# A four-layer graph network on one core: the bias of the norms on POOL, the normalisations split up, one set of transposes moved

## The chip, the cores and the metric

The kernel runs on one core of a Trainium2 chip. A core has a matrix engine (PE, with its weight loads shown apart as PEld), a vector engine (DVE), an activation engine (ACT), a general engine (POOL), and SyncE (SP), which starts transfers. Each has a queue of its own and takes its instructions strictly in the order in which they stand there; engines wait for each other by semaphores. The metric is the device time of one launch in microseconds (us), of which the median of three is taken.

## The reference, cut to what matters

There are 16 batches of 1024 nodes with 128 features (`x`) and an adjacency matrix of 1024 x 1024 (`adj`, about 1.6% of it non-zero). Four graph layers follow each other. Each begins with a norm over the 128 features and a ReLU, and adds its result to `x`:

```python
def _layernorm(x, axis=-1, eps=1e-5):
    m = jnp.mean(x, axis=axis, keepdims=True)
    v = jnp.var(x, axis=axis, keepdims=True)
    return (x - m) / jnp.sqrt(v + eps)

# --- layer 0 (adj_preln) ---
h = jnp.maximum(_layernorm(x, axis=-1), 0.0)
x = x + _L0_gnn_ref(h, adj, adj, L0_gnn_W, L0_gnn_b)
# --- layer 1 (adj_preln) ---
h = jnp.maximum(_layernorm(x, axis=-1), 0.0)
x = x + _L1_gnn_ref(h, adj, L1_gnn_W, L1_gnn_b)
# --- layer 2 (adj_preln) ---
h = jnp.maximum(_layernorm(x, axis=-1), 0.0)
x = x + _L2_gnn_ref(h, adj, ...)
# --- layer 3 (adj_preln) ---
h = jnp.maximum(_layernorm(x, axis=-1), 0.0)
x = x + _L3_gnn_ref(h, adj, L3_gnn_W, L3_gnn_a)
```

Layers 0 and 1 multiply by the adjacency matrix and a weight. Layer 2 is the heavy one: two rounds, each of which scores every edge with a small network over both of its nodes, adds up weighted messages, updates the nodes and normalises them (with weights `gamma` and `beta`; this norm ends the update and is not one of the four above). Layer 3 is an attention over the neighbours.

## The kernel before, in words

**Three lanes at once.** While the edge rounds of batch b run (the main lane, `main`), the attention of batch b - 1 is worked off beside them (`last`) and layers 0 and 1 of batch b + 1 (`first`), together with what main will need for it. Each lane is a Python generator that emits instructions and then yields a number; `weave` always takes next the lane that stands furthest behind, measured as the sum of its yielded numbers over its budget (`MAIN_US` 184, `FIRST_US` 115, `LAST_US` 70). A yield thus costs nothing on the chip: it only says where another lane's instructions may come in between, and a larger number puts the rest of the lane later. `layer0_own` is driven by a loop in `first` that charges 1.3 for every piece, whatever the piece itself yields. The framework beneath also moves an instruction ahead of others on its engine where it sees room for it, so the built order is near the emitted one but not the same. Once built, each engine's order is fixed.

**Data.** A batch's features are a tile of 128 partitions x 8 blocks x 128: 8 blocks of 128 nodes each. The edges are sorted into 36 buckets (pairs of node blocks, 28 off the diagonal and 8 on it), in 9 groups of 4. `build` makes four 0-1 matrices of a bucket (on, onT, om, omT) by a chain through one PSUM bank: PE turns (`pn`), ACT copies (`onT`), PE ranks (`pq`), DVE compares (`omT`), PE turns (`pm`), ACT copies (`om`). In the rounds, PE gathers by them (`pre`), ACT applies the ReLU (`hid`, line 1024), DVE keeps the remainder (line 1025), PE takes the dot products (`sc`), ACT the tanh (`srow`), and then DVE makes products (`val`) that PE scatters (`p`) and sums up as messages (`msg`).

**The norm.** `spread` makes the statistics of 8 blocks: 8 bn_stats on DVE and five small operations, then on POOL the power -1/2 of the variance (`rstd`, line 242). It returns the standard deviation's inverse, the *sum* of the two half means and a free row. `normal` makes from it the bias, -0.5 x sum x rstd, on DVE (line 249), and then normalises block by block on ACT, 8 activations with `rstd` as scale and the bias added (line 251). `pre_ln` emits the whole of it as one piece, then `transposed`: 8 transposes on PE (line 259) in two halves, each copied to SBUF by ACT (line 260). `layer0_own`, `layer1` and `layer3` begin with `pre_ln`; layer 2's norm is called in `first`, and `build` comes behind it. `update` uses `spread` too, for 4 blocks, and applies the result on DVE (lines 363 and 365).

So a norm is a chain DVE, POOL, DVE, ACT, PE, ACT, and each of its links stands in a queue with other lanes' work behind it. There are 64 such norms (4 in each of 16 batches) and 64 of `update`'s.

Of the kernel before, what the change touches and what calls it, by code (L numbers as in the profile page):

```python
# [13 lines left out]
AF = mybir.ActivationFunctionType  # L14
OP = mybir.AluOpType
# [36 lines left out]
def tile_four_gnn_layers(  # L52
# [22 lines left out]
    nc = tc.nc  # L75
# [106 lines left out]
    def flat(t):  # L182
        return t.rearrange("p t d -> p (t d)")

    def over_t(v, n=T):
        return v[:, None, :].to_broadcast([P, n, D])

    class Layers:
# [37 lines left out]
        def spread(self, src, name):  # L226

            n = src.shape[1]
            bn = self.small([P, T, 6], "bn", f"bn_{name}")[:, :n]
            for t in range(n):  # L230
                nc.vector.bn_stats(bn[:, t], src[:, t])

            st = self.small([P, 4, T], "stat", f"st_{name}")[:, :, :n]
            nc.vector.tensor_sub(st[:, 1], bn[:, :, 1], bn[:, :, 4])
            nc.vector.scalar_tensor_tensor(
                st[:, 2], bn[:, :, 2], D * LN_EPS, bn[:, :, 5], op0=OP.add, op1=OP.add
            )
            nc.vector.scalar_tensor_tensor(st[:, 1], st[:, 1], 0.25, st[:, 1], op0=OP.mult, op1=OP.mult)
            nc.vector.scalar_tensor_tensor(
                st[:, 1], st[:, 2], 1.0 / D, st[:, 1], op0=OP.mult, op1=OP.add  # L240
            )
            nc.gpsimd.tensor_tensor(st[:, 2], st[:, 1], half_neg[:, :n], op=OP.pow)  # L242
            nc.vector.tensor_add(st[:, 0], bn[:, :, 1], bn[:, :, 4])
            return st[:, 2], st[:, 0], st[:, 3]

        def normal(self, src, dst, func, name):

            rstd, mean2, less = self.spread(src, name)
            nc.vector.scalar_tensor_tensor(less, mean2, -0.5, rstd, op0=OP.mult, op1=OP.mult)
            for t in range(T):  # L250
                nc.scalar.activation(
                    dst[:, t], src[:, t], func, scale=rstd[:, t : t + 1], bias=less[:, t : t + 1]
                )

        def transposed(self, src, name, dst=None):
            dst = self.scratch(f"hT_{name}") if dst is None else dst
            for ts, ps in self.halves(f"tp_{name}"):
                for i, t in enumerate(ts):
                    nc.tensor.transpose(ps[:, i], src[:, t], ident)
                nc.scalar.activation(dst[:, ts[0] : ts[-1] + 1], ps, AF.Copy)  # L260
            return dst

        def pre_ln(self, xt, name, dst=None):

            h = self.scratch(f"h_{name}") if dst is None else dst
            self.normal(xt, h, AF.Relu, name)
            yield 2
            self.hT = self.transposed(h, name)
            yield 2

# [66 lines left out]
        def update(self, l, xf, xfT, msgT, dst, name):  # L337

            h2 = flat(self.scratch(f"h2s_{name}")).rearrange("p (k n) -> p k n", k=KB)
            for kb in range(KB):  # L340
                ps = self.one(f"h2_{name}_{kb}")
                for i, src in enumerate((xfT, msgT)):
                    nc.tensor.matmul(  # L343
                        ps, wu1_sb[:, l, i, kb * P : (kb + 1) * P], src,
                        start=(i == 0), stop=(i == 1),
                    )
                nc.scalar.activation(h2[:, kb], ps, AF.Relu, bias=bu1_sb[:, l, kb : kb + 1])
                yield 2
            new = self.scratch(f"xn_{name}")[:, :Q]
            ps = self.one(f"xn_{name}")  # L350
            for kb in range(KB):
                nc.tensor.matmul(
                    ps, wu2_sb[:, l, kb], h2[:, kb], start=(kb == 0), stop=(kb == KB - 1)
                )
            nc.scalar.activation(flat(new), ps, AF.Identity, bias=bu2_sb[:, l : l + 1])
            yield 2
            ps = self.one(f"tx_{name}").rearrange("p (t d) -> p t d", d=P)
            for t in range(Q):
                nc.tensor.transpose(ps[:, t], new[:, t], ident)
            nc.vector.tensor_add(dst, ps, xf)  # L360
            yield 1
            rstd, mean, _ = self.spread(dst, f"y_{name}")
            nc.vector.tensor_scalar(mean, mean, 0.5, None, op0=OP.mult)
            for t in range(Q):
                nc.vector.tensor_scalar(
                    dst[:, t], dst[:, t], mean[:, t : t + 1], rstd[:, t : t + 1],
                    op0=OP.subtract, op1=OP.mult,
                )
            yield 2
            nc.vector.tensor_mul(dst, dst, over_t(rows["gamma"][:, l], Q))  # L370
            nc.vector.tensor_add(dst, dst, over_t(rows["beta"][:, l], Q))
            yield 1
# [157 lines left out]
    class Edges:  # L530
# [197 lines left out]
        def first(self, b):  # L728
            s = self.next = Batch()
            lane, name = self.a, f"{b}"  # L730
            xt = self.work.tile([P, T, D], F32, tag="x", name=f"x_{b}")
            nc.sync.dma_start(xt, x[b].rearrange("(t p) d -> p t d", p=P))
            for _ in lane.layer0_own(xt, name):
                if b:
                    yield 1.3
            z, own = lane.z, lane.o
            yield 0


            s.adjT = self.dram.tile([N, N], F32, tag="adjT", name=f"adjT_{b}", bufs=3)  # L740
            has = self.work.tile([P, len(BUCKETS), P], FP8, tag="has", name=f"has_{b}", bufs=1)
            deg = self.work.tile([P, 2, T], F32, tag="deg", name=f"deg_{b}")
            rdeg = deg[:, 1]
            for t in range(T):
                at = self.load(
                    "a", adj[b, t * P : (t + 1) * P, :].rearrange("p (k n) -> p k n", n=P),
                    f"at_{b}_{t}",
                )
                ct = self.load("a", self.columns(adj[b], t), f"ct_{b}_{t}")
                turned = lane.scratch(f"tn_{b}_{t}")  # L750
                nc.scalar.activation(turned, at, AF.Copy, accum_out=deg[:, 0, t : t + 1])
                for ks, ps in lane.halves(f"tn_{b}_{t}"):
                    for i, k in enumerate(ks):
                        nc.tensor.transpose(ps[:, i], at[:, k], ident)
                    nc.scalar.activation(turned[:, ks[0] : ks[-1] + 1], ps, AF.Copy)
                    yield 1
                nc.sync.dma_start(self.columns(s.adjT, t), turned)
                parts = [(INDEX[t, t], t, t + 1)]
                if t + 1 < T:
                    parts.append((INDEX[t, t + 1], t + 1, T))  # L760
                for i, lo, hi in parts:
                    nc.vector.tensor_tensor(
                        has[:, i : i + hi - lo], ct[:, lo:hi], turned[:, lo:hi],
                        op=OP.logical_or, saturate=False,
                    )
                nc.vector.reciprocal(rdeg[:, t : t + 1], deg[:, 0, t : t + 1])
                lane.layer0_tile(t, ct, z, own, rdeg, name)
                yield 2
            lane.layer0_end(xt, own)
            self.count(s, has, name)  # L770
            yield 2
            yield from lane.layer1(
                xt, lambda t: self.load("a", self.columns(s.adjT, t), f"l1_{b}_{t}"), rdeg, name
            )
            s.xf = self.work.tile([P, T, D], F32, tag="xf0", name=f"xf0_{b}", bufs=1)
            yield from lane.pre_ln(xt, f"2_{name}", dst=s.xf)
            s.xT = self.kept(lane.hT, "xT", f"xT0_{b}")
            s.x = self.kept(xt, "x", f"xk_{b}")
            yield from self.build(s, has, name)

        def count(self, s, has, name):

# [49 lines left out]
                )  # L832
            return ps

        def build(self, s, has, name):

# [2 lines left out]
            for g, grp in enumerate(GROUPS):  # L841
# [3 lines left out]
                for i, tu in enumerate(grp):  # L845
                    b = INDEX[tu]
# [5 lines left out]
                rank = self.work.tile([P, Q, P], F16, tag="rank", name=f"rank_{name}_{g}")  # L852
                nc.scalar.activation(rank, pr, AF.Copy)
                yield 0.5
                for i, (t, u) in enumerate(grp):
                    nm = f"{name}_{t}_{u}"
                    on = self.rows_hot(s, t, u, nm)
# [6 lines left out]
                    for k in range(ck):  # L864
# [7 lines left out]
                        op=OP.is_equal, saturate=False,  # L872
# [570 lines left out]
```

## Time and profile before

| | |
|---|---|
| Time, median of 3 | 5407.02 us (5398.09 to 5412.55) |
| Span of the profiled run | 5411.4 us |
| Instructions | 113484 |
| POOL's power on 128x8 (line 242) | 64, 1.635 us in the median |
| The same on 128x4, in `update` | 64, 1.006 us |
| The bias on DVE (line 249) | 64, 0.167 us |
| A normalisation on ACT (line 251) | 512, 0.48 us |
| A steady batch | 328 us |

How it is read: the page gives each engine's busy time as a share of the span. Matmuls are pipelined and their ends are modelled, so a PE that is busy isn't necessarily at its peak; but where PE is *idle* in a kernel that PE bounds, time is lost. A group's row gives the line, the engine, the operation with its output and inputs, how often it ran, its busy time and mean, and behind the bar the idle time just before these instructions with what ended it. The windows give the busy time of each engine in a stretch.

### The profile page before, as it was taken

What the parts mean: (1) busy time and instruction counts of PE and PEld (TensorE: products, weight loads), DVE (VectorE), ACT (ScalarE), POOL (GpSimd) and SP (SyncE); (2) the same over time, 40 slices, a digit from 0 to 9 for tenths busy, and PEclk for the clock granted to TensorE, in tenths of its full rate; (3) what the DMA queues carried; (4) which work ended last, traced back from release to release, by engine and by line L of the source; (5) the groups of instructions that cost most, each with busy time, mean ns of one, the idle gap of its engine ahead of it and who ended that gap; (6) DMA issues with size and microseconds to landing.
All of it is one profiled execution on the core that took longest, in us unless ns stands there. A gap on an engine that the chain in (4) does not pass through costs nothing.

```text
span 5411.4 us, 113484 instructions
## 1 busy us (share of the span) xinstructions
PE 5012.4 (93%) x45109; PEld 3743.8 (69%) x45109; DVE 4288.8 (79%) x10567; ACT 3055.3 (56%) x6790; POOL 176.5 (3%) x137
## 2 busy tenths in 40 slices
PE   5999999999999999999999999999999999999986
PEld 4666767767776767767777677677767677677664
DVE  4776787877879788797877878778797787978876
ACT  4556464655646556465565656556465564655533
POOL 0000000000000000000000000000000000000000
PEclk8999999999999999999999999999999999999998
DMA  6242425243252423424234242432424334243121
GB/s 182 66 138 87 120 60 150 79 128 103 76 149 64 136 92 99 133 67 124 92 112 121 61 142 87 122 106 76 147 67 137 91 96 136 67 128 92 53 62 47
DMA packets 740139, 554.56 MB, mean 102 GB/s; under 512 B 32272, under 2 KB 686352, under 8 KB 739600
## 3 DMA queue, kind: packets, MB, share of 16 engines
q1 hardware_dynamic: 734496, 545.58, 33.6%
q8 instruction: 356, 5.83, 0.5%
q10 hardware_dynamic: 5104, 1.65, 0.1%
q14 instruction: 183, 1.50, 0.1%
HBM read 446.44 MB, written 100.66 MB: 101 GB/s over the span
## 4 chain that ended last, share of the span: by engine, by line
PE 61%; DVE 20%; ACT 10%; DMA 4%; POOL 2%; issue 2%; SPq 0%; ACTq 0%; POOLq 0%; DVEq 0%
PE pre L1008 15%; PE p L1120 7%; DVE val L1098 6%; PE nb L289 6%; PE msg L1137 5%; PE h L343 4%; PE hp L507 3%; PE bb L297 3%; PE sc L1041 3%; DVE hid L1025 3%; DMA at<-in_adj_dram 3%; PE pq L865 2%; PE pn L829 2%; POOL st L242 2%; ACT hid L1024 2%
## 5 line engine op out<-in xcount | busy, mean ns | idle before, releaser
L1024 ACT ACTIVATE hid<-pre 128x320 f16<-128x320 f32 (+1 forms) x2048 | 922.2, 456 | 713.5 <-PE pre L1008 679.5
L1025 DVE SCALAR_TENSOR_TENSOR hid<-pre,hid 128x320 f16<-128x320 f32 (+1 forms) x2048 | 1010.0, 505 | 262.7 <-ACT hid L1024 245.8
L1008 PEld LDWEIGHTS <-part 128*128 128x128 f16 x8192 | 752.7, 99 | 429.3 <-issue 211.4
L1008 PE MATMUL pre<-on,part 128*128 128x320 fp8e4 (+1 forms) x4096 | 966.6, 311 | 42.5 <-DVE hid L1025 32.3
L1008 PE MATMUL pre<-om,part 128*128 128x320 fp8e4 (+1 forms) x4096 | 979.0, 312 | 0.0
L1098 DVE TENSOR_TENSOR val<-onT,u 128x384 f32<-128x384 fp8e4 (+1 forms) x1152 | 603.3, 580 | 3.6
L1137 PE MATMUL msg<-upd,xf 128*128 128x128 f32 (+3 forms) x3008 | 591.8, 320 | 0.0
L1120 PE MATMUL p<-val,omT 128*128 128x128 f16 x6528 | 532.7, 219 | 31.6 <-DVE val L1098 27.2
L1120 PEld LDWEIGHTS <-omT 128*128 128x128 fp8e4 x6528 | 433.4, 96 | 109.6 <-issue 37.1
L1098 DVE TENSOR_TENSOR val<-omT,u 128x384 f32<-128x384 fp8e4 x896 | 442.7, 549 | 0.0
L1137 PEld LDWEIGHTS msg<-upd,xf 128*128 128x128 f32 x3008 | 411.6, 191 | 17.6 <-DVE upd L1128 0.9
L877 ACT ACTIVATE om<-pm 128x320 fp8e4<-128x320 f32 (+1 forms) x576 | 268.6, 466 | 274.5 <-PE pm L829 270.1
L1128 DVE SCALAR_TENSOR_TENSOR upd<-p,adj 128x512 f32<-128x512 f32 x512 | 349.0, 682 | 80.7 <-PE p L1120 76.7
L1120 PE MATMUL p<-val,onT 128*128 128x128 f16 x4480 | 370.9, 220 | 1.4 <-DVE upd L1128 1.4
L861 ACT ACTIVATE onT<-pn 128x384 fp8e4<-128x384 f32 (+1 forms) x576 | 298.4, 518 | 106.4 <-PE pn L829 98.4
L1062 ACT ACTIVATE srow<-sc,be_s,down 128x128 f32<-128x128 f32 (+2 forms) x512 | 256.3, 540 | 163.3 <-PE sc L1041 162.3
L507 PE MATMUL hp<-wh,e 128*128 128x129 f32 x2048 | 331.1, 287 | 16.7 <-DVE e L503 16.7
L1120 PEld LDWEIGHTS <-onT 128*128 128x128 fp8e4 x4480 | 305.2, 97 | 49.5 <-issue 14.9
L507 PEld LDWEIGHTS hp<-wh,e 128*128 128x128 f32 x2048 | 279.9, 195 | 51.5 <-issue 24.0
L1041 PE MATMUL sc<-hid,slide 128*32 128x320 f16 (+1 forms) x4096 | 272.4, 320 | 29.9 <-DVE hid L1025 28.5
L820 DVE TENSOR_SCALAR on<-far,wid 128x384 fp8e4<-128x384 f16 (+1 forms) x576 | 238.6, 427 | 60.0 <-PE pre L1008 52.2
L816 ACT ACTIVATE far<-iota_off,mid 128x384 f16<-128x384 f16 x448 | 275.6, 629 | 11.8 <-DVE on L820 11.3
(217 smaller groups left out, 8122.0 us busy)
## 6 DMA issues: line engine op xcount, KB each, us to landing
at<-in_adj_dram SPq DMA_DIRECT2D x128, 512.0 KB, 4.1
ct<-in_adj_dram SPq DMA_DIRECT2D x128, 512.0 KB, 4.5
adjT<-tn SPq DMA_DIRECT2D x128, 512.0 KB, 5.3
l<-adjT SPq DMA_DIRECT2D x128, 512.0 KB, 4.3
adj<-adjT SPq DMA_DIRECT2D x256, 256.0 KB, 3.5
a<-adjT SPq DMA_DIRECT2D x128, 384.0 KB, 3.2
adj<-adjT SPq DMA_DIRECT2D x448, 64.0 KB, 2.2
adj<-adjT SPq DMA_DIRECT2D x192, 128.0 KB, 2.9
```

The costliest lines, as they stand in the source:

```text
L289: nc.tensor.matmul(ps, mat[:, k], z[:, k], start=(k == 0), stop=(k == T - 1))
L507: nc.tensor.matmul(sums[:, t], e[:, i, t * P : (t + 1) * P], wh[:, k + i, : D + 1], start=False, stop=True, skip_group_check=True,)
L816: nc.scalar.activation(far[:, : ck * P], self.iota[t == u][:, : ck * P], AF.Abs, bias=s.mid[:, i : i + 1])
L861: nc.scalar.activation(onT, pn[:, : ck * P], AF.Copy, saturate=False)
L1008: nc.tensor.matmul(pre[:, :c], path.parts[node // Q][:, k, node % Q, v], hot[:, :c], start=(hot is on and k == 0), stop=(hot is om and k = ...
L1024: nc.scalar.activation(hid[:, 0, :c], pre[:, :c], AF.Relu)
L1025: nc.vector.scalar_tensor_tensor(hid[:, 1, :c], pre[:, :c], 0.0, hid[:, 0, :c], op0=OP.max, op1=OP.subtract)
L1041: ins = nc.tensor.matmul(self.sc[g * G : (g + 1) * G, : self.c], self.path.slide[:, self.l, G - 1 - r : 2 * G - 1 - r], self.hid[self.done ...
L1098: nc.vector.tensor_tensor(pair[:, i % 2, :ck], right[:, :ck], v.to_broadcast([P, ck, P]), op=OP.mult)
L1120: nc.tensor.matmul(self.ps[d][:, i], left[:, k], halves[:, k, :, h], start=(k, h) == terms[0], stop=(k, h) == terms[-1],)
L1128: nc.vector.scalar_tensor_tensor(upd, self.ps[d], S_SCALE, self.adj[:, d * Q : (d + 1) * Q], op0=OP.add, op1=OP.mult,)
L1137: nc.tensor.matmul(self.msg[h][:, (lo - h * Q) * P : (hi - h * Q) * P], self.xf[mb // Q][:, mb % Q], up, start=False, stop=True, skip_grou ...
```

## The change

It has three parts.

1. **The bias moves to POOL.** `spread` scales the sum of the means by -0.5 on DVE, so that it returns minus the mean; `normal` multiplies it by `rstd` on POOL, which has just made `rstd`, rather than on DVE, which would have to wait for it. `update` no longer scales the mean itself and adds it instead of subtracting.
2. **The normalisations are emitted by twos.** `normal` becomes a generator: it yields once behind the bias and once behind every second activation, so that other lanes' work can come between them. `pre_ln` passes these yields on.
3. **Layer 2's transposes wait.** In `first`, layer 2's norm is called directly, and its transposes (with the store of their result to DRAM) are handed to `build`, which emits them behind the first group of buckets. Batch 0, where nothing runs beside `build`, keeps its order. The copy of `x` to DRAM is emitted ahead of this norm.

```diff
@@ spread, normal
             nc.vector.tensor_add(st[:, 0], bn[:, :, 1], bn[:, :, 4])
+            nc.vector.tensor_scalar(st[:, 0], st[:, 0], -0.5, None, op0=OP.mult)
             return st[:, 2], st[:, 0], st[:, 3]
 
-        def normal(self, src, dst, func, name):
-
-            rstd, mean2, less = self.spread(src, name)
-            nc.vector.scalar_tensor_tensor(less, mean2, -0.5, rstd, op0=OP.mult, op1=OP.mult)
+        def normal(self, src, dst, name):
+
+            rstd, mean, less = self.spread(src, name)
+
+            nc.gpsimd.tensor_tensor(less, rstd, mean, op=OP.mult)
+            yield 0.5
             for t in range(T):
                 nc.scalar.activation(
-                    dst[:, t], src[:, t], func, scale=rstd[:, t : t + 1], bias=less[:, t : t + 1]
+                    dst[:, t], src[:, t], AF.Relu, scale=rstd[:, t : t + 1], bias=less[:, t : t + 1]
                 )
+                if t % 2:
+                    yield 0.4
@@ pre_ln
-            self.normal(xt, h, AF.Relu, name)
-            yield 2
+            yield from self.normal(xt, h, name)
             self.hT = self.transposed(h, name)
             yield 2
@@ update
             rstd, mean, _ = self.spread(dst, f"y_{name}")
-            nc.vector.tensor_scalar(mean, mean, 0.5, None, op0=OP.mult)
             for t in range(Q):
                 nc.vector.tensor_scalar(
                     dst[:, t], dst[:, t], mean[:, t : t + 1], rstd[:, t : t + 1],
-                    op0=OP.subtract, op1=OP.mult,
+                    op0=OP.add, op1=OP.mult,
                 )
@@ first
-            yield from lane.pre_ln(xt, f"2_{name}", dst=s.xf)
-            s.xT = self.kept(lane.hT, "xT", f"xT0_{b}")
             s.x = self.kept(xt, "x", f"xk_{b}")
-            yield from self.build(s, has, name)
+            yield from lane.normal(xt, s.xf, f"2_{name}")
+
+            def turn():
+                s.xT = self.kept(lane.transposed(s.xf, f"2_{name}"), "xT", f"xT0_{b}")
+
+            if not b:
+                turn()
+            yield from self.build(s, has, name, turn if b else None)
@@ build
+                if g == 1 and turn:
+                    turn()
+                    yield 2
```

More of the change, by code (lines that the diff above doesn't have):

```diff
@@ L833, in turned, with build @@
             return ps
-        def build(self, s, has, name):
+        def build(self, s, has, name, turn=None):
             s.on, s.onT, s.om, s.omT = {}, {}, {}, {}
```

## The prediction

> **What bounds the kernel now.** I read the page's engine shares first, then a steady stretch of one batch, then the groups on the bias's way (POOL, DVE, ACT), then who waited for the bias, and last the four places in one batch where a normalisation stands.
>
> ```profile
> PE 5012.4 (93%) x45109; PEld 3743.8 (69%) x45109; DVE 4288.8 (79%) x10567; ACT 3055.3 (56%) x6790; POOL 176.5 (3%) x137
> ```
> ```profile
> 1266.00:1594.00 328.00, 310.99 (x2822) 232.38 (x2818) 266.80 (x658) 190.44 (x424) 10.88 (x8) 0.98 0.35 105
> ```
>
> The second line is one batch of the steady part: 328 us in all, then busy PE, weight loads, DVE, ACT, POOL, then the granted clock (0.98) and the DMA share (0.35). PE is the bound: 311 of 328 us. So a gain can come only from the 17 us per batch in which PE stands still, and the question is how many of them belong to the norms. The groups:
>
> ```profile
> L242 POOL TENSOR_TENSOR st<-st,half_neg 128x8 f32<-128x8 f32 x64 | 105.4, 1646 | 2943.6 <-DVE st L239 2558.5 <-DVE whc L381 356.4 <-DVE st L243 21.9
> L242 POOL TENSOR_TENSOR st_y<-st_y,half_neg 128x4 f32<-128x4 f32 x64 | 69.7, 1089 | 2231.1 <-DVE st_y L239 1589.5 <-DVE st_y L363 641.6
> L249 DVE SCALAR_TENSOR_TENSOR st<-st 128x8 f32<-128x8 f32 x64 | 10.7, 167 | 98.1 <-POOL st L242 98.0
> ```
> Who waited for line 249, the bias:
> ```profile
>   ACT h L251: 96.0, 44
>   ACT xf L251: 21.2, 16
> ```
>
> The reader is to see a queue problem: a DVE instruction of 0.167 us stands at the head of DVE's queue for 1.5 us (98.0 us over 63 times) because POOL's power takes 1.646 us, and ACT's queue stands behind it for 2.0 us (117.2 us over 60 times). Eight normalisations then follow back to back. What PE loses at these places, in the batch from 938 to 1266 us (layers 2, 0, 3, 1 in that order; columns as above):
>
> ```profile
> 970.80:977.50 6.70, 3.55 (x22) 1.73 (x21) 4.39 (x25) 3.77 (x11) 2.95 (x2) 0.95 0.00 1
> 1107.50:1113.70 6.20, 4.61 (x62) 4.27 (x61) 3.60 (x10) 4.61 (x13) 1.64 (x1) 1.00 0.59 197
> 1210.50:1216.90 6.40, 4.29 (x44) 3.30 (x42) 4.96 (x16) 4.27 (x11) 1.64 (x1) 1.00 0.90 269
> 1237.50:1243.00 5.50, 4.27 (x32) 2.17 (x31) 1.09 (x6) 3.71 (x10) 1.64 (x1) 1.00 0.00 1
> ```
> ```profile
> PE tp L259 <- ACT xf L251: 2.4, 1, 2.4
> PE pq L865 <- ACT onT L861: 1.5, 1, 1.5
> PE p L1120 <- DVE val L1098: 1.4, 1, 1.4
> PE sc L1041 <- DVE hid L1025: 1.2, 1, 1.2
> ```
>
> In these 24.8 us PE is idle for 8.1 us, a third of the time, against 17 us in the whole batch of 328. The four longest PE waits there are the norm's: 2.4 us at layer 2 (its transposes, queued behind the normalisation), 1.5 at layer 0 (an onT copy behind the normalisation on ACT), 1.4 at layer 3 (a val product behind line 249 on DVE) and 1.2 at layer 1 (a hid remainder behind line 249 on DVE). Together 6.5 us per batch. The same places in the other steady batches lose the same to 0.2 us, so this is a property of the order and not of luck.
>
> **What the Trainium skill says.** "Perfetto Trace Analysis", section Optimizing Scalar/DVE Operations: where Scalar or Vector are not saturated but cause bubbles on other engines, breaking up work may let it be completed sooner. The trace agrees that this is the situation: ACT is 58% busy in the steady batch (190 of 328) and yet PE waits for it. "GPSIMD Engine Reference", section 3.1: a two-input elementwise operation on GpSimd takes about 2.6 cycles an element, at the 1.2 GHz of section 1. By it 8 elements are an estimated 0.02 us, so a small product is nearly all fixed cost; no run here shows one yet.[...] "Perfetto Trace Analysis", section GPSIMD Engine Instruction, calls POOL spans unreliable; here DVE starts 0.02 us after the reported end of the power, so I use them.
>
> **The change part by part.**
> Bias on POOL, 64 norms. Removed: line 249 on DVE, 0.167 us each, and its wait of 1.5 us at the head of DVE's queue. Added on DVE: the scaling of the mean in the helper, about 0.16 us, which waits for nothing from POOL. In the update the same scaling moves from line 363 (0.166 us) into the helper: nothing. So DVE's work stays and its 98 us of waiting go. Added on POOL: one 128x8 product. Its price is bounded below by the fixed part of the power: 8 elements 1.636 us and 4 elements 1.006, so 0.157 an element and 0.376 fixed; with the skill's 0.02 that is 0.4 us. It is bounded above by the power itself, 1.64. I take 0.45[...]; plus 0.1 for the wait between the two. For ACT the bias then comes 0.45 + 0.1 + hop after the power, instead of 0.19 (a line-249 start to ACT's start, as at 1239.53 to 1239.73): 0.4 us later (1.6 later at the upper bound). Queued behind ACT's first normalisation are the main path's hid activations, the bucket copies and the exponentials; PE waits for them.
>
> Normalisations by twos. Nothing is added: eight times 0.48 us as before. The built order of the changed kernel in the steady part shows what it does. Layer 0: the last step of the statistics on DVE stands ahead of two hid remainders, and ACT does five to seven other instructions before its first normalisation, which then go 4, 1, 3 with hid and bucket copies between. I expect its 1.5 us to go to 0.2. Layer 3: 4 and 4 with a hid between, and a hid and a turned copy (0.44 + 0.6 us) behind DVE's last step; DVE is free, so 1.4 goes to 0.6, a part of ACT's wait. Layer 1: 3, 3, 2 with the update's h2s and a hid between; DVE's hid no longer waits, but ACT still does, for about 2.4 us less what stands ahead of it: 1.2 goes to 0.8. Layer 2: 7 and 1, hardly split, and ACT waits some 1.5 us.
>
> Transposes behind the first group. In the order of before, PE has them directly behind the wait, woven with score and hidden matmuls that they hold up. In the changed order about 30 ACT instructions lie between the last normalisation and their copies, so they wait for nothing: the 2.4 us go. ACT's own wait is left: 0.7. The later store of the transposed features is read only at the next batch's start, more than 100 us on; hidden. The earlier store of x too.
>
> Sum: 6.5 becomes 2.3, so 4.2 us per batch. Fifteen batches are prepared or ended beside another: 15 x 4.2 = 63 us. The norms that run alone (three at the head, one at the end) get 0.4 us longer each: +1.5.
>
> The pacing. The first layers' lane now yields 5 pieces in each normalisation. Layer 0 charges 1.3 for every piece, so it goes from 6 pieces (7.8) to 10 (13.0); with the small rest the lane sums to 119.1 instead of 113.7, of a budget of 115. The main lane ends at 183.8/184 = 0.999. So the lane went from ending at 0.989 to 1.036, and 0.037 of a batch (12 us, some 3.5 diagonal buckets) is emitted after main has ended. In the built order this hardly shows: ACT has 32 rows from main's last hid to the last bucket's copy, 27 before, and the next batch's first hid stands 24 rows behind, 25 before. I charge 0.6 us per batch, 9 us; the bounds are 0 and half of the 12.
>
> Total: -63 + 1.5 + 9 = -52; 5407 - 52 = 5355.
>
> **The rivals.**
> *The wait only changes hands*: DVE is freed, but ACT holds the same things up for 0.4 us longer, and PE's waits for val and hid become waits for ACT. For it: three of the four norms still have a first normalisation close behind the statistics. Against: layers 0 and 2 account for 3.9 of the 6.5 us, and there the order clearly changes. If only layer 0 and half of layer 2 are gained and the pacing costs 1.5 us: 15 x (2.7 - 1.5) = 18, less 1.5: about 5390; with less, no change.
> *The late lane costs more than the norms gain (slower)*: a bucket alone is a chain PE, ACT, PE, DVE, PE, ACT through one PSUM bank. If half of the 12 us is idle PE, 6 us a batch against 4.2: 15 x 1.8 = 27, about 5434. For it: the lane now overruns its budget. Against: the order at the seam is nearly the same.
> *Everything is recovered*: all 6.5, nothing lost, and some bucket waits (pm, pn and pq, each 0.5 to 1.2 us) shrink with a freer DVE: 15 x 7.5 = 112, about 5295. For it: DVE's 98 us of waiting fall in the busiest stretches. Against: POOL's 1.65 us remains and ACT has to sit through it somewhere.
>
> **How the numbers follow.** Forecast 0.57, changes hands 0.15, slower 0.18, all recovered 0.10. Faster by over 0.3% is below 5391: the forecast nearly whole (0.54), all recovered, and some of the second case: 0.70. Slower, above 5423: 0.17. Within: 0.13. The range reaches down to 5295, the best case, and up to 5425, which takes in changed hands and a part of the slower one.
>
> **What will show it.** In the changed profile: no DVE wait for POOL at a 128x8 statistic (98 us before); a POOL product of about 0.45 us, 64 times; ACT's wait for the bias near 100 us, now for POOL; PE's wait for the transposes of xf (38.5 us over 15 on PE, 51.2 over 42 on weight loads) almost gone; PE busy unchanged near 5012 while the span falls; a steady batch of about 324.5 us. I am wrong if the POOL product costs as much as the power, if the transposes turn up as a wait elsewhere, or if new waits in the bucket chain (pn, pq, pm) at a batch's end outgrow 4 us a batch.

## The result, and the profile after

The changed kernel takes 5437.12 us in the median, where the kernel before took 5403.70 beside it: a ratio of 1.0063, with a 95% interval of 1.005 to 1.0076. It is slower by 33 us; 5355 was forecast. First come the engine shares from the page of the changed kernel, then one steady batch and the four norms in it, in the columns of before (busy PE, weight loads, DVE, ACT, POOL, granted clock, DMA share):

```profile
PE 5001.8 (92%) x45109; PEld 3752.1 (69%) x45109; DVE 4284.2 (79%) x10567; ACT 3066.4 (56%) x6790; POOL 198.9 (4%) x201
```
```profile
2126.70:2457.20 330.50, 309.46 (x2820) 232.36 (x2818) 266.74 (x658) 190.76 (x425) 12.61 (x12) 0.99 0.35 105
2203.30:2210.00 6.70, 6.63 (x67) 5.54 (x66) 6.43 (x20) 5.05 (x16) 2.28 (x2) 1.00 0.77 229
2246.00:2253.20 7.20, 5.60 (x27) 2.46 (x27) 3.04 (x7) 4.49 (x11) 2.15 (x2) 1.00 0.00 0
2303.40:2311.90 8.50, 4.88 (x33) 2.48 (x30) 6.43 (x18) 4.97 (x12) 2.31 (x2) 0.80 0.00 0
2332.50:2341.00 8.50, 8.35 (x88) 6.91 (x88) 7.85 (x23) 8.26 (x23) 1.84 (x2) 1.00 0.43 141
```

The first line is the batch: 330.5 us. PE works no more than before (309.5 us); it stands still for 21 us of the batch. The four other lines are the norms of layers 3, 1, 2 and 0. At layers 3 and 0 PE is now nearly gapless. At layers 1 and 2 it still stands still for 1.6 and 3.6 us. The next lines show who waits there, then POOL's rows, then who waited for the bias, which is now made on line 251 of the changed kernel:

```profile
PE tp L264 <- ACT h L254: 1.5, 1, 1.5
PE msg L566 <- DVE part L906: 2.1, 1, 2.1
```
```profile
L242 POOL TENSOR_TENSOR st<-st,half_neg 128x8 f32<-128x8 f32 x64 | 110.0, 1719 | 1565.6 <-DVE st L244 1194.6 <-DVE st L239 342.4 <-DVE deg L769 16.3
L251 POOL TENSOR_TENSOR st<-st 128x8 f32<-128x8 f32 x64 | 22.0, 344 | 5.0
```
```profile
  ACT h L254: 80.3, 32
  ACT xf L254: 46.4, 16
```

DVE no longer waits for POOL at a norm's statistics. ACT does: 126.7 us over 48 times, a little more than the 117.2 of before. The product costs 0.20 us in the median. The transposes of xf have left the list of large waits of PE, but two others have come in their place. Here is the list over the whole execution, one line from before and two from the changed kernel:

```profile
PE tp L259 <- ACT h L251: 28.4, 4, 12.2
```
```profile
PE tp L264 <- ACT h L254: 52.4, 20, 12.3
PE msg L566 <- DVE part L906: 28.9, 14, 2.1
```

The transposes of the other layers' norms (`h`) now hold PE up 20 times instead of 4: that is layer 1's 1.5 us, batch by batch. The prediction had named this as a sign of being wrong, transposes that turn up as a wait elsewhere. And PE's zeroing of a message bank waits for DVE's `part`, which it did not do before. What stands around this second wait, in the timeline of the changed kernel at layer 2's norm:

```profile
2303.25 0.47 DVE L231 BATCH_NORM_STATS2 bn<-x 128x6 f32<-128x128 f32 x2
...
2304.08 0.60 ACT L905 ACTIVATE part<-bb 128x512 f16<-128x512 f32 x1 [2.33 <-DVE bb L904]
...
2304.96 0.68 DVE L906 TENSOR_TENSOR part<-bb,part 128x512 f16<-128x512 f32 x1
2305.11 1.64 POOL L242 TENSOR_TENSOR st<-st,half_neg 128x8 f32<-128x8 f32 x1 [13.65 <-DVE st L244]
...
2305.70 0.61 PE L566 MATMUL msg<-iota,zero 128*128 128x512 f16 x1 [2.07 <-DVE part L906]
...
2306.83 0.67 POOL L251 TENSOR_TENSOR st<-st 128x8 f32<-128x8 f32 x1
...
2307.53 0.88 ACT L254 ACTIVATE xf<-x,st 128x128 f32<-128x128 f32 x2 [2.85 <-POOL st L251]
```

Layer 2's statistics (bn and what follows it) stand on DVE among the steps with which main prepares its second round (lines 904 to 906), whose end frees the bank that PE wants. Then ACT stands still for 2.85 us for the bias. The norm has landed where main's two rounds meet; whether that costs anything is tried below.

### The profile page after: what moved, and what is told of

Its sections match the earlier page's. It is cut to its first block, busy times and chain, and to the rows that moved or that the text cites. A ratio compares the mean times of both kernels' runs of the same rounds, so it can differ in the third digit from the quotient of the medians.

```text
span 5443.3 us, 113453 instructions
## 1 busy us (share of the span) xinstructions
PE 5001.8 (92%) x45109; PEld 3752.1 (69%) x45109; DVE 4284.2 (79%) x10567; ACT 3066.4 (56%) x6790; POOL 198.9 (4%) x201
## 4 chain that ended last, share of the span: by engine, by line
PE 48%; DVE 29%; ACT 12%; DMA 6%; issue 3%; POOL 3%; SPq 0%; ACTq 0%; POOLq 0%; DVEq 0%
PE pre L1020 12%; DVE val L1110 9%; PE p L1132 5%; PE nb L293 5%; DVE hid L1037 4%; PE msg L1149 4%; DMA at<-in_adj_dram 3%; PE sc L1053 3%; PE h L347 3%; PE bb L301 3%; ACT hid L1036 2%; PE hp L510 2%; DMA a<-adjT 2%; PE pn L838 2%; PE pq L877 2%
## 5 line engine op out<-in xcount | busy, mean ns | idle before, releaser
L1149 PEld LDWEIGHTS msg<-upd,xf 128*128 128x128 f32 x3008 | 413.8, 193 | 12.7 <-DVE upd L1140 1.5
L1132 PE MATMUL p<-val,onT 128*128 128x128 f16 x4480 | 384.9, 220 | 4.0 <-DVE upd L1140 4.0
L881 DVE TENSOR_TENSOR omT<-pq,odd_off 128x384 fp8e4<-128x384 f32 x448 | 247.7, 553 | 83.9 <-PE pq L877 81.0
```

Of the source, the lines that this page charges most:

```text
L1132: nc.tensor.matmul(self.ps[d][:, i], left[:, k], halves[:, k, :, h], start=(k, h) == terms[0], stop=(k, h) == terms[-1],)
L1149: nc.tensor.matmul(self.msg[h][:, (lo - h * Q) * P : (hi - h * Q) * P], self.xf[mb // Q][:, mb % Q], up, start=False, stop=True, skip_grou ...
```

## The experiments

Three theories ran against each other: the pacing costs (the lane's later place), the wait only changes hands, or the parts cost something where they were put. All times are set against the kernel before, measured beside each; behind a ratio stands its 95% interval. First each part alone.

**The bias alone on POOL** (`p1_bias`):
```diff
-            nc.vector.scalar_tensor_tensor(less, mean2, -0.5, rstd, op0=OP.mult, op1=OP.mult)
+            nc.gpsimd.tensor_tensor(less, rstd, mean, op=OP.mult)
```


> The bias on POOL alone, emitted where it was, no other part of the change. Theory A (the late lane costs; the parts for the norms themselves gain): DVE's 98 us of waiting for POOL go, about half of PE's waits for val and hid at layers 1 and 3 goes, so 15 x 1.5 = 20 us faster than before, about 5383. Theory B (the wait only changes hands to ACT, which stands still longer): no gain or a loss, 5400 to 5440.


5410.19 us, ratio 1.0017 (1.001 to 1.0024). It is slower by 9 us. PE's waits behind DVE fell, as hoped: for the products `val` from 27.2 to 6.9 us, of `sc` for `hid` from 28.5 to 11.8. But ACT's wait for the bias rose from 117.2 to 138.1 us, PE's wait of `pre` for `hid` from 32.3 to 56.0, and that for the transposes of `h` from 28.4 us over 4 times to 40.4 over 18. The wait changed hands here. The product itself explains little of it: ACT's first normalisation starts 0.32 us behind the end of the power in the median, instead of 0.24, which makes some 5 of the 21 us that ACT waits longer. Where the rest comes from is not shown.

**The normalisations by twos alone** (`p2_twos`: the yields of the changed kernel's `normal`, nothing else).


> The normalisations emitted by twos alone, with the pacing that comes with them (the first layers' lane sums to 119.1), bias still on DVE, transposes where they were. Theory A: the pacing's loss is in it (about 5 us a batch) and little of the gain, so 5440 to 5470. Theory B: no loss from the pacing, 5390 to 5410.


5437.18 us, 1.0069 (1.0056 to 1.0083): as slow as the whole change. But the pacing is in it, since layer 0's extra pieces are charged here too; the run `pace_up` below has the pacing without the pieces.

**The transposes alone** (`p3_turn`: the third part's diff).


> Layer 2's transposes behind the first group alone; pacing as before (lane sums to 113.7). Theory A: PE's 2.4 us wait for them goes and nothing else changes, so up to 15 x 2 = 30 us faster, about 5375. Theory C (the transposes in the bucket chain's only PSUM bank cost there what they gained): 5400 to 5440.


5401.71 us, 1.0001 (0.9993 to 1.0009). PE's wait for them fell from 38.5 to 5.0 us over the span, as forecast, and nothing was gained. Other waits of PE grew by as much: that of `p` for `val` from 27.2 to 40.5 us, and that of `sc` for `hid` from 28.5 us over 22 times to this:
```profile
PE sc L1050 <- DVE hid L1034: 62.4, 34, 2.6
```
In the bucket chain, where the expectation looked for the cost, only one small wait is new, that of `pn` for the copies of the transposes: 7.1 us.

**The pacing alone** (`pace_up`):
```diff
                 if b:
-                    yield 1.3
+                    yield 13.0 / 6
```


> The kernel before with one number changed: each of layer 0's 6 pieces is charged 2.17 instead of 1.3, so that the first layers' lane sums to 118.9 as in the changed kernel (119.1) and overruns its budget by as much. Theory A: this alone loses 4 to 8 us a batch, 5460 to 5520 (the gains of the norms are not in it). Theory B or C: within 0.3% of before, 5390 to 5420.


5432.53 us, 1.0065 (1.0051 to 1.0079). No instruction is added, removed or moved to another engine; one number that is only a lane's pace costs 32 us, about as much as the whole change lost. PE's waits for `omT` (27.9 to 57.4 us), for `val` (27.2 to 56.2) and for the transposes of `h` (28.4 to 48.1) grew, and the new one of the changed kernel is there too:
```profile
PE msg L563 <- DVE part L894: 34.6, 14, 2.6
```

**The change without the pacing** (`after_paced`, the changed kernel with `yield 7.8 / 10`).


> The changed kernel with layer 0's ten pieces charged 0.78 each instead of 1.3, so that the lane sums to 113.9 as before. Theory A (the pacing is the whole loss, the three parts gain): 5340 to 5385. Theory D (the pacing is the whole loss, and the three parts gain nothing of their own, as the bias alone at 1.0017 and the transposes alone at 1.0001 suggest): 5390 to 5415. Theory E (the loss stays, since it sits in the norms): about 5435.


5413.14 us, 1.0024 (1.0015 to 1.0033): 24 us below the changed kernel (20, when each is taken against the kernel before beside it), and yet no faster than before. The timeline of this kernel at layer 2's norm, and its longest wait of PE over the whole execution, show what has become of the norm's wait there:
```profile
2285.15 1.64 POOL L242 TENSOR_TENSOR st<-st,half_neg 128x8 f32<-128x8 f32 x1 [30.15 <-DVE st L244]
...
2287.34 3.19 ACT L254 ACTIVATE xf<-x,st 128x128 f32<-128x128 f32 x8 [2.65 <-POOL st L251]
...
2290.43 0.73 ACT L1074 ACTIVATE srow<-sc,be_s,down 128x480 f32<-128x480 f32 x1
...
2291.21 0.69 PE L1086 MATMUL pt<-ident,srow 128*128 128x128 f32 x2 [3.70 <-ACT srow L1074]
```
```profile
PE pt L1086 <- ACT srow L1074: 53.1, 16, 3.7
```
ACT waits 2.65 us and then does all eight normalisations in a row. The transposes no longer hold PE up; the tanh (srow) behind the normalisations on ACT does, for 3.70 us, where before PE lost 2.4 in the same place. Over the whole execution PE waits 53.1 us for this tanh, against 1.2 before; the transposes of xf had cost 38.5.

**Is it the overrun at the end of the lane?** The budget was changed in the changed kernel (`after_budget`: `FIRST_US = 120.5`) and in the one before (`budget_110`, `budget_120`).


> The changed kernel with the lane's budget 120.5 instead of 115: its 119.1 end at 0.988 of the main lane as before, but everything behind layer 0 still stands later in it (layer 2's norm at 0.573 of main, where before it was at 0.555 and in the changed kernel at 0.600). Theory F (the overrun at the end costs): like the paced kernel, the loss gone. Theory G (where the norms and updates meet costs): only a part of the loss goes, 5410 to 5430.


5469.98 us, 1.0130 (1.0115 to 1.0146).


> The kernel before with the lane's budget 110 instead of 115: it ends at 1.034 of main, an overrun as in the changed kernel, but layer 2's norm stands at 0.580 only. Theory F: slower by 25 to 40 us, about 5435. Theory G: less, 5410 to 5420, or no loss.


5424.31 us, 1.0050 (1.0036 to 1.0063).


> The kernel before with the lane's budget 120: it ends at 0.948 of main, layer 2's norm at 0.532. Theory F: no overrun before or now, 5395 to 5410. Theory H (any shift of the lanes against each other moves the time by about half a per cent, either way, since the positions of the waits are drawn anew): off by 15 us or more in either direction.


5365.48 us, 0.9934 (0.9921 to 0.9948), the fastest of all versions that compute the norm. The changed kernel without an overrun is the slowest of all, so the overrun is not the cause. Two more runs of the kernel before shift only a part of the lane:
```diff
# shift_late
             self.count(s, has, name)
-            yield 2
+            yield 7.2
# shift_early: layer 0 as in pace_up, and
                 lane.layer0_tile(t, ct, z, own, rdeg, name)
-                yield 2
+                yield 1.35
```


> The kernel before, with the lane's one piece between layer 0 and layer 1 charged 7.2 instead of 2: layer 0 stands where it was, layers 1, 2 and the buckets stand as late as in the changed kernel (119 in all). Theory G (it is the later place of layer 2's norm and the buckets against main's seam that costs): 5425 to 5445, as with layer 0's pieces charged more. If it is layer 0's pace that costs: 5395 to 5410.


5405.56 us, 1.0003 (0.9994 to 1.0011).


> The reverse: layer 0's pieces charged 2.17 as in the changed kernel, and each of its eight adjacency tiles 0.65 less, so that layers 1 and 2 and the buckets stand where they stood before (113.7 in all). Theory G: 5395 to 5415. If it is layer 0's pace that costs: 5425 to 5445.


5402.54 us, 0.9999 (0.9991 to 1.0008). Neither the late place of layers 1, 2 and the buckets nor layer 0's slow pace costs by itself; both together do (`pace_up`). In `shift_late` the new wait at the seam is there too (34.5 us over 14), but it is paid back elsewhere. So no single place explains the pacing; my theory of the seam, the place where main's rounds meet, fell.

**What the wait for POOL is worth.** Here every engine's order is kept, and only POOL's power is replaced by a cheaper operation of the same shape, in the 64 norms, so that their result is not the norm:
```diff
-            nc.gpsimd.tensor_tensor(st[:, 2], st[:, 1], half_neg[:, :n], op=OP.pow)
+            nc.gpsimd.tensor_tensor(st[:, 2], st[:, 1], half_neg[:, :n], op=OP.mult if n == T else OP.pow)
```


> The kernel before, with every engine's order kept, and in the 64 norms (not in the updates) POOL's power replaced by a product of the variance with -0.5: the norm itself is not computed then, only the duration differs, 1.64 us against about 0.2. Theory W (POOL's 1.64 us at the head of DVE's and ACT's queues is what PE loses at the norms): 1.44 us less in each of 64, PE follows, 60 to 90 us faster, 5310 to 5340. Theory N (the norms' waits are covered or come back elsewhere): less than 25 us.


5309.32 us, 0.9825 (0.9811 to 0.9838). The power fell to 0.2 us, ACT's wait for the bias from 117.2 to 33.4 us, and a steady batch to 321.6 us:
```profile
L242 POOL TENSOR_TENSOR st<-st,half_neg 128x8 f32<-128x8 f32 x64 | 13.5, 212 | 2936.3 <-DVE st L239 2554.3 <-DVE whc L381 357.3 <-DVE st L243 21.9
```
```profile
610.00:931.60 321.60, 309.37 (x2829) 231.96 (x2829) 268.06 (x661) 190.51 (x425) 5.14 (x8) 0.99 0.36 107
```
Not all of the 93.5 us that this takes off are waits of PE:
```profile
PE 4988.1 (94%) x45109; PEld 3725.2 (70%) x45109; DVE 4292.0 (81%) x10567; ACT 3054.3 (58%) x6790; POOL 84.8 (2%) x137
```
Between the two profiled executions the span fell by 100 us (5411.4 to 5311.0): PE's idle time by 76 (399 to 323), and its busy time by 24 (5012.4 to 4988.1), with a mean granted clock of 0.984 against 0.978. Whether the shorter power brings that part about, or the other values that PE then multiplies, is not shown.


> The same replacement in the changed kernel, again with its order kept; the norm is not computed. If its norms had been freed from the wait, as I forecast, nothing or up to 15 us. If the wait is still there and only stands before ACT (theory W: ACT waits 127 us for the bias), 60 to 90 us faster, 5345 to 5375.


5398.43 us, 0.9994 (0.9988 to 1.0001). Now two effects can be told apart. Against the kernel before beside them, before_short lies at -93.5 us, after_short at -4.4, and the changed kernel at +33.4. So shortening the power is worth 93.5 us in the kernel before and 33.4 + 4.4 = 37.8 in the changed one, 55.7 less. And the changed order is slower by 93.5 - 4.4 = 89.1 us when the power is short in both. (That 89.1 - 55.7 gives back the 33.4 follows from how the two are formed; it confirms nothing.) PE's idle time in the profiled executions tells the same with smaller numbers: the short power takes 76 us of it before, and 34 in the changed kernel (441.6 to 407.8).

Where the 89 us are is seen in PE's longest waits, in before_short and then in after_short:
```profile
PE pre L1008 <- DVE hid L1025: 33.4, 55, 2.8
PE pm L829 <- DVE omT L869: 27.5, 39, 1.7
...
PE sc L1041 <- DVE hid L1025: 12.3, 8, 1.8
```
```profile
PE pre L1020 <- DVE hid L1037: 59.1, 92, 2.8
PE sc L1053 <- DVE hid L1037: 50.0, 63, 2.6
PE pm L838 <- DVE omT L881: 44.4, 50, 2.6
PE msg L566 <- DVE part L906: 29.0, 14, 2.1
```
They are spread over the hid remainders, the buckets and the message bank: PE comes to other engines' results a little too early in many places. Which edit makes them was tried with the short power too (again without the norm's result).

> The changed kernel with layer 0's pieces charged 0.78 (the lane sums to 113.9, as before), its order kept, and POOL's power in the norms replaced by a product (the norm is not computed). Theory R (the pacing makes most of the 89 us by which the changed order is slower when the power is short in both): 5310 to 5335, near the 5309 of the kernel before with the short power. Theory S (the three parts' own order costs it): 5360 to 5390.


5349.17 us, 0.9907 (0.9892 to 0.9922).


> The kernel before with only layer 0's charge raised to 2.17, order kept, and the short power (the norm is not computed). Theory R: the pacing costs the same or more without the waits for POOL, 5370 to 5400. Theory S: 5310 to 5340.


5356.70 us, 0.9918 (0.9904 to 0.9931).


> The kernel before with layer 2's transposes behind the first group alone, and the short power (the norm is not computed). If the transposes' new place is what costs: 5340 to 5355. If not: 5305 to 5320.


5320.75 us, 0.9846 (0.9833 to 0.9860).


> The kernel before with the bias on POOL and the normalisations by twos, layer 0 paced (0.78), transposes where they were, and the short power (the norm is not computed). If the bias and the pieces cost: 5340 to 5355. If the transposes do: 5305 to 5320. If both are half: 5325 to 5335.


5333.98 us, 0.9869 (0.9853 to 0.9886).

| kernel | against before, us | with the short power, us | the power's price, us | slower than before_short by, us |
|---|---|---|---|---|
| before | 0 | -93.5 | 93.5 | 0 |
| transposes alone (p3) | +0.8 | -80.8 | 81.6 | 12.7 |
| bias and twos, paced (p12) | not measured | -67.6 | | 25.9 |
| all three, paced | +13.5 | -51.2 | 64.7 | 42.3 |
| pacing alone | +31.7 | -43.6 | 75.3 | 49.9 |
| the change | +33.4 | -4.4 | 37.8 | 89.1 |

The power's price is the difference of the two columns ahead of it. In the last column, transposes 12.7 and bias and twos 25.9 make 38.6, against 42.3 for all three paced; with the pacing's 49.9 that is 92.2, against 89.1. By the intervals each figure is uncertain by some 10 us, so this agrees with costs that add up, and doesn't prove it; the transposes' 12.7 is only just clear of nothing. The column of prices has a warning too: the pacing alone, which edits nothing in the norms, already lowers the price from 93.5 to 75.3. A wait for POOL can also become cheaper because PE loses its time elsewhere.

**Can ACT's remaining wait be covered?** The paced changed kernel, with the pause behind the bias at 2.4 instead of 0.5 and that behind the transposes at 0.1 instead of 2:


> The changed kernel, paced (0.78), with the lane's pause between the bias and the first normalisation 2.4 instead of 0.5, taken from the pause behind the transposes, so that the sum stays. If other lanes' ACT work comes in between, ACT's wait for the bias (151 us in the paced kernel) falls by half and the time to 5350 to 5385. If the framework moves the normalisations forward again, nothing: 5400 to 5420.


5367.83 us, 0.9940 (0.9926 to 0.9954). ACT's wait for the bias fell from 150.6 to 101.8 us. This version does the whole computation and beats both kernels; so does budget_120. But PE's wait for the tanh is as long as in the paced kernel (55.9 us, 53.1 there), so the gain is not at that place; its whole order has moved too, and how much of the 32 us comes from the shorter wait of ACT is not shown.


> The same with the lane's budget 120 (which took 34 us off the kernel before). If place and wait are separate costs, 30 us below the former; if the gain at 120 was one place of the waits among many, anywhere from 5360 to 5430.


5386.79 us, 0.9973 (0.9963 to 0.9984). ACT waits 97.0 us for the bias, and yet the two gains do not add up: the budget of 120, a gain of 34 us in the kernel before, costs 19 here.

## Why the prediction was wrong

The forecast was -52 us, the result +33: 85 us apart. With the pacing undone (`after_paced`) the rest of the change stands at +13.5, where the prediction's terms for it give -61.5, so 75 of the 85 lie in the three parts and some 11 in the pacing. Term by term:

*PE is the bound, and the norms' waits cost it 6.5 us a batch.* Right in kind. That the short power gave 93.5 us, and 15 batches at 6.5 make 97.5, is in part luck: PE's idle time in a steady batch fell from 17.0 to 12.2 us, which is 4.8, and some of the 93.5 us is busy time of PE.

*Bias on POOL: a product of 0.45 us, ACT's bias 0.4 us later.* The product was 0.20, below the bound of 0.4 that I had taken from the power's fixed part: what one operation costs beside its elements is no floor for another. ACT's start behind the power came 0.1 us later in the median and 0.3 in the mean, not 0.4. DVE's wait went, as said. But alone this part lost 9 us: I had counted freed DVE as gain and its price to ACT as an aside.

*The norms: 6.5 us become 2.3, 63 us over all.* The direction was right, the size too large. The power's price fell by 55.7 us from the kernel before to the changed one, but by 28.8 when the pacing is undone (93.5 to 64.7), and by 37.5 against the pacing alone (75.3 to 37.8). ACT's wait for the bias did not fall: 126.7 us, and 150.6 when paced, against 117.2. By layers, PE's waits at the norm: layer 0 0.2 forecast, none left in the list; layer 3 0.6 forecast, none left; layer 1 0.8 forecast, 1.5 measured; layer 2 0.7 forecast, but 2.1 for DVE's `part` in the changed kernel and 3.7 for the tanh when paced. (Layer 0's norm has also moved: its first normalisation stands over 120 us ahead of its first transpose, where before it was 20.) At layer 2 I priced only the transposes' own wait. What holds PE up there when paced is ACT's queue, and the next instruction of PE that needs ACT waits at least as long.

*Normalisations by twos, "nothing is added"; transposes hidden.* This step failed: I priced these edits by what they do at the norm and took all other places as unchanged, so the prediction puts them at nothing. With the short power the three parts' order costs 42.3 us without the pacing (38.6 as the sum of its parts). That is more than the 28.8 by which they lower the power's price, and the difference is the +13.5.

*The pacing: 0.6 us a batch, since the built order at the seam hardly differs.* This term was mis-sized: 9 us forecast, with bounds of 0 and 90, and 32 measured on the kernel before, 20 within the change, 47 to 50 with the short power. I looked at one seam of a lane whose every later place had moved by 5 of 115 parts, and took a like order there for a like order.

*The rivals.* The slower one gave 5434, close to the 5437 measured, but for a cause that the runs refute: the overrun is not what costs (after_budget has none and takes 5470; shift_late has it and takes 5406). That nearness is luck. That the wait changes hands is right for the bias alone. That everything is recovered is far off: in the changed kernel the power still costs 37.8 us.

It is shown that the pacing costs 20 to 50 us, by what it is set against, and that the waits it makes are many small ones of PE for DVE and ACT. Not settled is why this place of the lanes is bad and those of shift_late and shift_early are not: paces and budgets alone, with no instruction changed, gave times from 5365 to 5433 for the kernel before and from 5413 to 5470 for the changed one (5368 with its pauses moved), and no rule from place to time came out of it. A cut of the power's 1.64 us that keeps the result was not measured.

## What to carry to other kernels

Price a change in a kernel of woven lanes in two terms: what it does at the place that it means, and what it does to everything that is emitted after it. The first can be read from waits; for the second, count every yield or pause that the edit adds, and expect a spread as wide as that of a shift of the lanes without any other change (here 0.7% either way, from budget_120 to pace_up). Keeping the lane's sum as it was gave 20 of the 33 us back here, but not the rest. To learn what a wait is worth, replace the slow operation by a cheap one of the same shape and keep the order: the answer has none of the second term in it. It holds for that order alone: here it was 93.5 us in one and 37.8 in another. And where an in-order engine stands before a result, moving away one instruction that waits for it frees nothing if the next one needs the same engine (the transposes' 38.5 us became the tanh's 53.1). What should help is other work ahead of the waiting instruction on the engine that waits; `late_acts` tried it and was faster, but PE's wait for the tanh stayed, so this is not shown yet.

## What the runs showed of the hardware

On POOL a product of 128x8 took 0.20 us and the power 1.64, though both are one two-input instruction on 8 elements a partition. The power on 4 elements took 1.006, so an estimate from these two sizes is 0.157 us an element and 0.38 fixed: most of the power's price is in its elements, and even its fixed part is larger than the whole product. Where the product reads the power's result directly behind it, its reported span varied from 0.20 to 0.67 us; it started 0.08 us behind the reported end of the power each of the 64 times. In the kernel before, DVE's bias had started 0.03 us behind that end (the prediction has 0.02).
